# Two graph layers on one core: where the products of the first linear stand among those of the aggregate

## The chip, the cores and the metric

The kernel runs on one core of a Trainium2 chip. The metric is the device time of one execution in microseconds. Before the change the median of three runs is 2444.21 us (2444.15 to 2444.86).

## The reference, cut to what matters

The input x has 16 batches of 1024 rows and 256 channels, all in float32. Layer 0 is an attention over a weighted graph, with a residual and a layer normalisation; the change does not touch it. Layer 1, on its result x, is:

```python
A_norm = A + jnp.eye(n)
deg = A_norm.sum(0) + A_norm.sum(1) - jnp.diagonal(A_norm)
dinv = rsqrt(deg)
A_hat = A_norm * dinv[:, None] * dinv[None, :]
agg = jnp.einsum('nm,bmd->bnd', A_hat, x)          # the aggregate
h   = relu(batchnorm(agg @ W1.T + b1))             # the first linear: 256 -> 512
out = batchnorm(h @ W2.T + b2)                     # the second linear: 512 -> 256
x   = layernorm(x + out)
```

The batch normalisations take their statistics over all 16 x 1024 rows, so h can be scaled only once the first linear of every batch is done.

## The kernel before, in words

The kernel first works through layer 0, then through layer 1 in three stages: aggregate and first linear of every batch; second linear of every batch; normalisation, residual and output. The change lies in the first of these, the loop at L1636 over the batches b = 1 to 15. (The aggregate of batch 0 is made earlier, by `aggregate_first`; the linear of batch 15 comes after the loop, as plain products, L1673 to L1690.)

Both the aggregate and the linear are made with seven products in place of eight (the Strassen-Winograd scheme). `products` (L637) writes it once for both: three accumulating banks of PSUM, called a, b and c, and seven steps, in the order p1, p6, p2, p7, p5, p4, p3. Each step is some matmuls and the reading of the bank afterwards by one instruction:

- p1: bank a, then ScalarE copies it (L656). p2 adds to bank a, and ScalarE copies it to the first quarter of the output (L667 in the aggregate, L669 with a bias in the linear).
- p6: bank b, then an add on VectorE (L646 in the aggregate, L648 in the linear). p7 and p4 add to bank b, each followed by another such add.
- p5 and p3, on bank c:

```python
def p5():
    t["c"] = bank(f"c_{name}")
    mm(5, t["c"], True)
    nc.vector.tensor_add(out[3], t["c"], t["u3"])    # L679

def p3():
    mm(3, t["c"], False)                             # adds to the same bank
    nc.vector.tensor_add(out[1], t["c"], t["u2"])    # L687
```

A product that adds to a bank has to come after the instruction that read it.

In the aggregate (`aggregate`, L1541, matmuls at L1558) a step has four matmuls 128x128 by 128x512 in float32; each shows as two MATMUL records in the profile. Its left operands are the batch's x1l and sums of it, x1S, which GpSimd makes two batches ahead (`x1_sums`, L1533, at L692 to L695), when the aggregate that last used the buffer has ended. In the linear (`linear1`, L1566, matmuls at L1590) a step has one such matmul, and there are two groups g of seven steps for each batch: 14 products. After each group come four batch statistics on VectorE (L1599), and after the second the store of h to DRAM from GpSimd's queue (L1602). Before any of its products, `linear1(b)` issues four sums of the aggregate's result on VectorE, called tT (`right_sums`, L697, at L699 to L702); the p4, p5, p6 and p7 of the linear use them.

What sets the order: on TensorE, ScalarE and VectorE the order of instructions is the order in which the Python code issues them (`manual_schedule`, L1508); each engine works through its own queue. In the loop, each step of the aggregate of batch b is followed by products of the linear of batch b - 1, taken from the list `lin` by `run_linear(lin, k)` (L1622): k products, then whatever stands in the list before the next product (statistics, the store). Behind the aggregate's last step, p3, the loop calls `linear1(b)` for the next pass, and with it the four sums, and only then `run_linear`. In batch 1 the apply step of the last layer normalisation (`last_apply`), the last store of x1 and the load and sums of batch 2 follow the aggregate's first step. After batch 1 VectorE also computes the range of the denominators (L1608 to L1611), and after batch 2 one small matmul (L1615) follows.

PSUM has eight banks of 128x512 here, given out in turn (`bank`, L1519); the temporaries of the linear have one buffer each (`temps("h")`), tT and x1S two.

Of the kernel before, what the change touches and what calls it, by code (L numbers as in the profile page):

```python
# [515 lines left out]
def fast_path(  # L516
# [120 lines left out]
    def products(name, bank, out, mm, temps, bias):  # L637

        t = {}

        def add(dst, ps, src, b):
            if b is None:
                nc.vector.tensor_add(dst, ps, src)  # L646
            else:
                nc.vector.scalar_tensor_tensor(dst, ps, b, src, op0=ALU.add, op1=ALU.add)  # L648

        up, low = bias or (None, None)  # L650

        def p1():
            t["a"] = bank(f"a_{name}")
            mm(1, t["a"], True)
            t["p1"] = temps("p1", name)
            nc.scalar.copy(t["p1"], t["a"])  # L656

        def p6():
            t["b"] = bank(f"b_{name}")
            mm(6, t["b"], True)  # L660
            t["u2"] = temps("u2", name)
            add(t["u2"], t["b"], t["p1"], up)

        def p2():
            mm(2, t["a"], False)
            if up is None:
                nc.scalar.copy(out[0], t["a"])  # L667
            else:
                nc.scalar.activation(out[0], t["a"], AF.Identity, bias=up)  # L669

        def p7():
            mm(7, t["b"], False)
            t["u3"] = temps("u3", name)
            add(t["u3"], t["b"], t["p1"], low)
# [6 lines that stand above are left out]
        def p4():  # L681
            mm(4, t["b"], False)
            add(out[2], t["b"], t["p1"], low)

        def p3():
            mm(3, t["c"], False)
            nc.vector.tensor_add(out[1], t["c"], t["u2"])  # L687

        return [p1, p6, p2, p7, p5, p4, p3]
# [7 lines left out]
    def right_sums(eng, T, b11, b12, b21, b22):  # L697

        eng.tensor_tensor(T[0], b12, b11, ALU.subtract)  # L699
        eng.tensor_tensor(T[1], b22, T[0], ALU.subtract)  # L700
        eng.tensor_tensor(T[2], b22, b12, ALU.subtract)
        eng.tensor_tensor(T[3], b21, T[1], ALU.subtract)  # L702
# [32 lines left out]
    with (  # L735
# [545 lines left out]
        def load_x1l(b):  # L1281
            x1l[b] = xp.tile([P, NCH, C], F32, tag="x", name=f"x1l_{b}")
            nc.sync.dma_start(x1l[b], x1_chunks[b])
# [28 lines left out]
        with tc.manual_schedule(  # L1312
# [70 lines left out]
            for j in range(len(bursts)):  # L1383
                b, u = j // PERB, j % PERB
# [127 lines left out]
    with (  # L1512
# [9 lines left out]
        def temps(k):  # L1522
            return lambda key, name: strt.tile([P, HALF], F32, tag=f"{key}{k}", name=f"{key}_{name}")
# [9 lines left out]
        def x1_sums(b):  # L1533
            x1S[b] = strs.tile([P, 4, NCH // 2, P], F32, tag="x1S", name=f"x1S_{b}")
            xt = x1l[b]
            left_sums(
                nc.gpsimd, [x1S[b][:, i] for i in range(4)],
                xt[:, M0, C0], xt[:, M1, C0], xt[:, M0, C1], xt[:, M1, C1],
            )

        def aggregate(b):  # L1541
            pool, tag = (aggp, "agg") if b % 2 else (xTp, "xT")
            t = agg[b] = pool.tile([P, CC, N], F32, tag=tag, name=f"agg_{b}")
            xt, S, aT = x1l[b], x1S[b], aht["T"]

            def mm(k, ps, start):
                for i in range(NCH // 2):
                    lo, hi = aht[i], aht[i + NCH // 2]
                    left, right = {
                        1: (xt[:, i, C0], lo[:, H0]),  # L1550
                        2: (xt[:, i + NCH // 2, C0], hi[:, H0]),
                        3: (S[:, 3, i, :], hi[:, H1]),
                        4: (xt[:, i + NCH // 2, C1], aT[:, 3, i, :]),
                        5: (S[:, 0, i, :], aT[:, 0, i, :]),
                        6: (S[:, 1, i, :], aT[:, 1, i, :]),
                        7: (S[:, 2, i, :], aT[:, 2, i, :]),
                    }[k]
                    nc.tensor.matmul(  # L1558
                        ps, left, right, start=(start and i == 0), stop=(i == NCH // 2 - 1),
                        skip_group_check=True,  # L1560
                    )

            out = (t[:, 0, H0], t[:, 0, H1], t[:, 1, H0], t[:, 1, H1])
            return products(f"agg{b}", bank, out, mm, temps("a"), None)

        def linear1(b):  # L1566
            t = agg.pop(b)
            ht = hp.tile([P, HC, N], F32, tag="h", name=f"hw_{b}")
            tT = strs.tile([P, 4, HALF], F32, tag="tT", name=f"tT_{b}")
            right_sums(  # L1570
                nc.vector, [tT[:, i, :] for i in range(4)],
                t[:, 0, H0], t[:, 0, H1], t[:, 1, H0], t[:, 1, H1],
            )
            steps = []
            for g in range(2):
                up, low = g, 2 + g

                def mm(k, ps, start, g=g):
                    f0 = slice(g * P, (g + 1) * P)
                    f1 = slice(C + g * P, C + (g + 1) * P)  # L1580
                    left, right = {
                        1: (w1T[:, 0, f0], t[:, 0, H0]),
                        2: (w1T[:, 1, f0], t[:, 1, H0]),
                        3: (wS[:, 3, f0], t[:, 1, H1]),
                        4: (w1T[:, 1, f1], tT[:, 3, :]),
                        5: (wS[:, 0, f0], tT[:, 0, :]),
                        6: (wS[:, 1, f0], tT[:, 1, :]),
                        7: (wS[:, 2, f0], tT[:, 2, :]),
                    }[k]
                    nc.tensor.matmul(ps, left, right, start=start, stop=True, skip_group_check=True)  # L1590

                places = ((up, H0, 0), (up, H1, 1), (low, H0, 0), (low, H1, 1))
                out = [ht[:, k, hs] for k, hs, _ in places]
                bias = (cols["b1"][:, up : up + 1], cols["b1"][:, low : low + 1])
                steps += products(f"h{b}_{g}", bank, out, mm, temps("h"), bias)

                def stats(places=places, out=out):
                    for (k, _, half), o in zip(places, out):
                        nc.vector.bn_stats(bn1_st[:, k, 2 * b + half, :], o)  # L1599

                steps.append(stats)
            steps.append(lambda: nc.gpsimd.dma_start(h_d[b], ht))  # L1602
            return steps
# [18 lines left out]
        def run_linear(steps, k):  # L1622
            while steps and k:
                name = steps[0].__name__
                steps.pop(0)()
                k -= name.startswith("p")
            while steps and not steps[0].__name__.startswith("p"):
                steps.pop(0)()
# [4 lines left out]
            w1T[:, 0, F0], w1T[:, 1, F0], w1T[:, 0, F1], w1T[:, 1, F1],  # L1633
        )
        lin = linear1(0)
        for b in range(1, B):  # L1636
            if 1 < b < B - 1:
                load_x1l(b + 1)
                x1_sums(b + 1)
            elif b == B - 1:  # L1640
                h0 = []
                for i in range(2):
                    t = xp.tile([P, 2, N], F32, tag="x", name=f"hl_0_{i}")
                    nc.sync.dma_start(t, h_d[0][:, 2 * i : 2 * i + 2, :])
                    h0 += [t[:, 0, :], t[:, 1, :]]
            steps = aggregate(b)
            for i, step in enumerate(steps):
                step()
                if i == len(steps) - 1 and b < B - 1:
                    later = linear1(b)  # L1650
                if b > 1 or i > 0:
                    run_linear(lin, 3 if b == 1 and i in (3, 5) else 2)
                if b == 1 and i == 0:
                    last_apply()
                    nc.scalar.dma_start(x1_chunks[B - 1], x_last)
                    load_x1l(2)
                    x1_sums(2)
            lin = later
            if b == 1:
                denominators_range()  # L1660
            if b == 2:
                denominators_good()
# [399 lines left out]
```

## Time and profile before

| What | Value |
| --- | --- |
| median of three runs | 2444.21 us |
| the profiled execution | 2444.04 us |
| its span, first to last instruction | 2442.3 us |
| busy TensorE, VectorE, ScalarE, GpSimd | 98%, 76%, 51%, 19% of the span |
| mean granted TensorE clock | 0.997 |
| the loop of batches 1 to 15 | 1593.15 to 2140.74 us |
| distance of two batches in it, from batch 4 on | 36.42 us |

The busy shares are averages over the whole span. A line of the profile gives an instruction's line in the kernel (L1590), the engine, the tile written and the tiles read (`b_h<-tT,wS`: bank b of the linear, from tT and wS), and durations in us. In names, `a_agg`, `b_agg` and `c_agg` are the banks of the aggregate, `a_h`, `b_h` and `c_h` those of the linear; `u_h` and `p_h` are its temporaries, `hw` its output. PEld is TensorE's loading of weights, which runs beside its matmuls. A matmul's end is modelled, so the distance of two starts says more than a duration.

### The profile page before, as it was taken

What the parts mean: (1) busy time and instruction counts of PE and PEld (TensorE: products, weight loads), DVE (VectorE), ACT (ScalarE), POOL (GpSimd) and SP (SyncE); (2) the same over time, 40 slices, a digit from 0 to 9 for tenths busy, and PEclk for the clock granted to TensorE, in tenths of its full rate; (3) what the DMA queues carried; (4) which work ended last, traced back from release to release, by engine and by line L of the source; (5) the groups of instructions that cost most, each with busy time, mean ns of one, the idle gap of its engine ahead of it and who ended that gap; (6) DMA issues with size and microseconds to landing.
All of it is one profiled execution on the core that took longest, in us unless ns stands there. A gap on an engine that the chain in (4) does not pass through costs nothing.

```text
span 2442.3 us, 32486 instructions
## 1 busy us (share of the span) xinstructions
PE 2401.4 (98%) x12294; PEld 1015.7 (42%) x12294; DVE 1860.5 (76%) x2561; ACT 1239.0 (51%) x1539; POOL 462.8 (19%) x467
## 2 busy tenths in 40 slices
PE   9999999999999999999999999999999999999996
PEld 5343443443434434434344343344444444444444
DVE  5688878878888788788888888955566556479978
ACT  7376675765765756657657667420110111144568
POOL 0021112111211211112112112422122122010026
PEclk9999999999999999999999999999999999999999
DMA  5124232332242332332322326321221221265558
GB/s 164 40 40 87 56 50 70 69 52 65 41 81 57 49 79 61 53 70 53 66 62 40 87 46 92 90 103 69 86 103 69 88 102 69 86 222 177 180 202 357
DMA packets 437877, 221.96 MB, mean 91 GB/s; under 512 B 361552, under 2 KB 411216, under 8 KB 431568
## 3 DMA queue, kind: packets, MB, share of 16 engines
q1 hardware_dynamic: 418400, 169.20, 28.2%
q0 software_dynamic: 2528, 33.57, 3.3%
q10 hardware_dynamic: 16784, 17.04, 2.1%
q8 instruction: 98, 1.61, 0.3%
q14 instruction: 67, 0.55, 0.1%
HBM read 136.06 MB, written 83.69 MB: 90 GB/s over the span
## 4 chain that ended last, share of the span: by engine, by line
PE 86%; DVE 9%; ACT 2%; DMA 1%; issue 1%; POOL 0%; POOLq 0%; DVEq 0%; ACTq 0%
PE ps L1053 18%; PE po L1074 18%; PE pgb L885 7%; PE b_agg L1558 4%; PE pga L885 4%; PE c_agg L1558 4%; PE pk L982 4%; PE b_o L1766 3%; PE pv L995 3%; PE a_agg L1558 2%; PE b_h L1590 2%; PE pgc L885 2%; PE pgd L885 2%; PE c_o L1766 2%; PE a_o L1766 2%; PE c_h L1590 2%
## 5 line engine op out<-in xcount | busy, mean ns | idle before, releaser
L1058 ACT ACTIVATE p<-ps 128x1024 f32<-128x1024 f32 x512 | 497.2, 1021 | 183.8 <-PE ps L1053 146.0
L1084 DVE TENSOR_TENSOR acc<-acc,p 128x1024 f32<-128x1024 f32 x384 | 499.9, 1302 | 53.4 <-ACT p L1058 28.5
L1053 PE MATMUL ps<-qT,kT 64*64 64x512 f32 x4096 | 488.1, 592 | 0.3 <-ACT p L1058 0.3
L1074 PE MATMUL po<-p,v 64*64 64x512 f32 x4096 | 485.3, 589 | 0.0
L1149 POOL TENSOR_TENSOR o<-o,r_all 128x512 f32<-128x512 f32 x62 | 94.8, 1540 | 1162.3 <-DVE r_all L1143 989.0
L1074 PEld LDWEIGHTS po<-p,v 64*64 64x64 f32 x4096 | 158.2, 133 | 281.2 <-issue 274.3
L1053 PEld LDWEIGHTS ps<-qT,kT 64*64 64x64 f32 x4096 | 151.5, 133 | 286.8 <-issue 249.1
L836 DVE SCALAR_TENSOR_TENSOR wg<-wg,adj_s 128x1024 f32<-128x1024 f32 x128 | 149.6, 1216 | 17.6 <-ACT wg L832 17.6
L827 ACT ACTIVATE wg<-crow,ccol 128x1024 f32<-128x1024 f32 x128 | 146.8, 1147 | 0.0
L832 ACT ACTIVATE wg<-wg 128x1024 f32<-128x1024 f32 x128 | 136.0, 1062 | 0.9
L995 PE MATMUL pv<-kvw_s,xT 128*128 128x256 f32 x512 | 125.1, 387 | 0.0
L982 PE MATMUL pk<-xT,kvw_s 128*128 128x512 f32 x256 | 121.9, 598 | 3.1 <-ACT drow L1128 3.1
L995 PEld LDWEIGHTS pv<-kvw_s,xT 128*128 128x128 f32 x512 | 95.7, 191 | 50.3 <-issue 14.2
L895 ACT ACTIVATE qT<-qT 128x512 f32<-128x512 f32 x60 | 37.4, 630 | 156.1 <-DVE qT L898 145.3
L885 PE MATMUL pgb<-wg,S 128*128 128x512 f32 x240 | 111.0, 605 | 0.0
L885 PE MATMUL pga<-wg,x 128*128 128x512 f32 x240 | 109.6, 599 | 0.7 <-ACT qT L908 0.7
L1558 PE MATMUL a_agg<-ahT,x1l 128*128 128x512 f32 x240 | 108.1, 593 | 0.7 <-ACT agg L1300 0.7
L1150 POOL TENSOR_TENSOR x<-x,o 128x512 f32<-128x512 f32 x62 | 107.8, 1749 | 2.4
L1558 PE MATMUL b_agg<-aT,x1S 128*128 128x512 f32 x240 | 107.9, 592 | 0.0
L656 ACT COPY p_agg<-a_agg 128x512 f32<-128x512 f32 x15 | 8.8, 585 | 183.4 <-PE a_agg L1558 183.4
L692 POOL TENSOR_TENSOR x1S<-x1l 128x512 f32<-128x512 f32 x15 | 19.4, 1297 | 353.6 <-PE c_agg L1558 349.6
L1082 DVE TENSOR_TENSOR acc<-p,p 128x1024 f32<-128x1024 f32 x64 | 77.3, 1208 | 7.5 <-ACT p L1058 7.5
(230 smaller groups left out, 3468.5 us busy)
## 6 DMA issues: line engine op xcount, KB each, us to landing
h<-hw POOLq DMA_DIRECT2D x16, 2048.0 KB, 6.7
hl<-h SPq DMA_DIRECT2D x32, 1024.0 KB
x<-x ACTq DMA_DIRECT2D x16, 1024.0 KB
x1l<-x SPq DMA_DIRECT2D x16, 1024.0 KB
xf<-x SPq DMA_DIRECT2D x16, 1024.0 KB
o<-oS SPq DMA_DIRECT2D x62, 256.0 KB
o<-o SPq DMA_DIRECT2D x248, 64.0 KB
x<-in_x_dram SPq DMA_DIRECT2D x15, 1024.0 KB
```

What stands on the lines that cost most here:

```text
L827: nc.scalar.activation(w, s["crow"], AF.Abs, bias=s["ccol"][:, n : n + 1])
L832: nc.scalar.activation(w, w, AF.Tanh, scale=0.5)
L836: nc.vector.scalar_tensor_tensor(w, w, 1.0, adj_s[:, n, :], op0=ALU.subtract, op1=ALU.mult)
L885: nc.tensor.matmul(ps, left, right, start=(start and i == 0), stop=(i == NCH // 2 - 1), skip_group_check=True,)
L982: nc.tensor.matmul(ps, kvw_s[:, c, kc * P : (kc + 1) * P], s["xT"][:, c, hs], start=(c == 0), stop=(c == CC - 1),)
L995: nc.tensor.matmul(pt[:, j * C : (j + 1) * C], s["xT"][:, c, n * P : (n + 1) * P], kvw_s[:, c, C : 2 * C], start=(c == 0), stop=(c == CC - 1),
L1053: nc.tensor.matmul(ps[kh * D : (kh + 1) * D, hd * HALF : (hd + 1) * HALF], kT[r, pr, ks], qT[r, pr, qh * HALF : (qh + 1) * HALF], start=Tr ...
L1058: nc.scalar.activation(p, ps, AF.Exp)
L1074: nc.tensor.matmul(g["po"][kh][hd * D : (hd + 1) * D, :], s["v"][r, m, h * D : (h + 1) * D], p[r, hd * HALF : (hd + 1) * HALF], start=(m = ...
L1084: nc.vector.tensor_add(g["acc"], g["acc"], p)
L1558: nc.tensor.matmul(ps, left, right, start=(start and i == 0), stop=(i == NCH // 2 - 1), skip_group_check=True,)
L1766: nc.tensor.matmul(ps, left, right, start=(start and i == 0), stop=(i == 1), skip_group_check=True,)
```

## The change

Only the number of the linear's products behind each of the seven steps of the aggregate is changed. Before, no product followed the first step of batch 1, three followed its fourth and sixth, and two every other step. After, the counts are written out: a row for batch 1 and a row for all later batches. The sum is 14 in each, as before.

| behind the aggregate's | p1 | p6 | p2 | p7 | p5 | p4 | p3 |
| --- | --- | --- | --- | --- | --- | --- | --- |
| batch 1, before | 0 | 2 | 2 | 3 | 2 | 3 | 2 |
| batch 1, after | 0 | 1 | 2 | 3 | 2 | 3 | 3 |
| later batches, before | 2 | 2 | 2 | 2 | 2 | 2 | 2 |
| later batches, after | 1 | 2 | 2 | 2 | 2 | 2 | 3 |

In the later batches the products of the first group are p1 / p6, p2 / p7, p5 / p4, p3 behind the first four steps, and those of the second p1, p6 / p2, p7 / p5, p4, p3 behind the last three. Before, it was p1, p6 / p2, p7 / p5, p4 / p3 with the second group's p1 / p6, p2 / p7, p5 / p4, p3.

```diff
         lin = linear1(0)
+        counts = ((0, 1, 2, 3, 2, 3, 3), (1, 2, 2, 2, 2, 2, 3))
         for b in range(1, B):
...
             steps = aggregate(b)
             for i, step in enumerate(steps):
                 step()
                 if i == len(steps) - 1 and b < B - 1:
                     later = linear1(b)
                 if b > 1 or i > 0:
-                    run_linear(lin, 3 if b == 1 and i in (3, 5) else 2)
+                    run_linear(lin, counts[b > 1][i])
                 if b == 1 and i == 0:
                     last_apply()
```

## The prediction

> **What bounds the kernel now.** I read the page first, then the chain of waits, then TensorE's timeline through the stage that the change touches, then VectorE's beside it.
>
> ```profile
> span 2442.3 us, 32486 instructions
> PE 2401.4 (98%) x12294; PEld 1015.7 (42%) x12294; DVE 1860.5 (76%) x2561; ACT 1239.0 (51%) x1539; POOL 462.8 (19%) x467
> PE 86%; DVE 9%; ACT 2%; DMA 1%; issue 1%; POOL 0%; POOLq 0%; DVEq 0%; ACTq 0%
> ```
>
> TensorE (PE) is busy 98% of the span, so the question is only where it still waits, and where it will wait. The loop over batches 1 to 15 runs from the first aggregate product at 1593.15 us to the plain products at 2140.74 us: 547.6 us. A step of four aggregate products takes 3.43 us (1740.42 to 1743.86), so one product takes 0.858 us; the 28 + 14 of a batch take 42 x 0.858 = 36.05 us. In TensorE's timeline the starts of successive batches lie 36.42 us apart from batch 4 on: 0.37 us too much. The same timeline shows where it goes (columns: start, duration, instruction):
>
> ```profile
> 1749.01 1.02 PE L1590 MATMUL a_h<-agg,w12T 128*128 128x512 f32 x2
> 1750.14 1.13 PE L1590 MATMUL b_h<-tT,wS 128*128 128x512 f32 x2
> 1751.10 1.45 PE L1558 MATMUL a_agg<-ahT,x1l 128*128 128x512 f32 x3
> ```
>
> p2 of the linear starts at 1749.01, so p7 is due at 1749.87. It starts at 1750.14, and what follows starts 0.96 us later instead of 0.86: 0.37 us lost. The list of waits names the cause, the add of p6:
>
> ```profile
> PEld b_h L1590 <- DVE u_h L648: 13.5, 13, 2.3
> ```
>
> VectorE (DVE) reaches that add late, because of what stands ahead of it in its queue:
>
> ```profile
> 1738.91 0.69 DVE L687 TENSOR_TENSOR agg<-c_agg,u_agg 128x512 f32<-128x512 f32 x1 [2.74 <-PE c_agg L1558]
> 1739.63 1.14 DVE L699 TENSOR_TENSOR tT<-agg 128x512 f32<-128x512 f32 x1
> 1740.81 1.64 DVE L700 TENSOR_TENSOR tT<-agg,tT 128x512 f32<-128x512 f32 x1
> 1742.37 1.75 DVE L701 TENSOR_TENSOR tT<-agg 128x512 f32<-128x512 f32 x1
> 1744.05 1.75 DVE L702 TENSOR_TENSOR tT<-agg,tT 128x512 f32<-128x512 f32 x1
> 1745.72 0.74 DVE L648 SCALAR_TENSOR_TENSOR hw<-b_h,col_b,p_h 128x512 f32<-128x512 f32 x1
> 1746.38 0.67 DVE L687 TENSOR_TENSOR hw<-c_h,u_h 128x512 f32<-128x512 f32 x1
> 1746.98 2.46 DVE L1599 BATCH_NORM_STATS2 bn_st<-hw 128x6 f32<-128x512 f32 x4
> 1749.36 0.73 DVE L648 SCALAR_TENSOR_TENSOR u_h<-b_h,col_b,p_h 128x512 f32<-128x512 f32 x1
> ```
>
> From the add that ends the aggregate (L687) VectorE works without a gap: four right sums for the next batch (1739.63 to 1745.72, 6.09 us), two adds, four statistics, and only then the late add at 1749.36. In this order nothing that TensorE needs early stands behind the sums. In batch 14 the sums are short, and no wait follows:
>
> ```profile
> 2103.90 0.69 DVE L699 TENSOR_TENSOR tT<-agg 128x512 f32<-128x512 f32 x1
> ...
> 2106.44 0.74 DVE L648 SCALAR_TENSOR_TENSOR hw<-b_h,col_b,p_h 128x512 f32<-128x512 f32 x1
> ```
>
> **What the Trainium skill says.** "PSUM — Partial Sum Buffer", section "Engine vs sequencer instructions": VectorE's queue is strictly first in, first out, and matmuls complete in program order. The trace agrees: the add at 1749.36 starts only when the statistics end. "SBUF — State Buffer", "Who interferes with whom": a VectorE instruction with two SBUF inputs contends with a GpSimd instruction that reads SBUF. The trace agrees: the sums take 1.14 to 1.75 us each beside GpSimd's x1S sums (1738.97 to 1745.24), and 0.68 to 0.69 us in batch 14, where GpSimd has none. "TensorE: Matmul & The Clock Gate", Part 1: TensorE's clock halves after an idle window of about 3.4 us and returns after a busy one; Part 4 adds that transposes don't count as busy in the same way. The trace shows one such drop, in the last stage (columns: stretch, length, busy of five engines, granted clock, DMA):
>
> ```profile
> 2352.20:2355.60 3.40, 1.11 (x8) 0.92 (x8) 2.56 (x7) 3.29 (x3) 0.55 (x1) 1.00 0.93 390
> 2355.60:2356.00 0.40, 0.00 (x0) 0.00 (x0) 0.27 (x1) 0.40 (x1) 0.00 (x0) 0.68 0.92 389
> 2358.00:2359.00 1.00, 1.00 (x2) 0.23 (x1) 0.99 (x3) 1.00 (x1) 0.00 (x0) 0.50 0.00 0
> 2359.00:2359.40 0.40, 0.40 (x3) 0.20 (x2) 0.38 (x2) 0.40 (x2) 0.00 (x0) 0.80 0.00 0
> ```
>
> After 2.88 us of idle time behind a few transposes the clock is 0.50 from about 2355.7 to 2359.1, some 3.4 us, and a pair that otherwise takes 1.02 us takes 1.84.
>
> **The change part by part.** No instruction is added or removed; products of the linear move, with the adds and copies that they issue, past products of the aggregate. The order of instructions of the changed kernel shows it on TensorE and VectorE; on SyncE and GpSimd the order stays, and so do the store of h, at the end of the linear, and the loads of x1l.
>
> 1. p6 moves from behind the aggregate's p1 to behind its p6. Its add then ends by about 10.6 us of the batch (below) and p7, now behind the aggregate's p2, is due at 15 x 0.858 = 12.9: the wait goes. Worth 1.76 us in batch 2 (where VectorE also does the range of the denominators: p7 starts 1.66 late and loses 0.10 on restarting), 0.33 in batch 3, 0.37 x 11 = 4.07 in batches 4 to 14: 6.2 us. Batch 15 has none now.
>
> 2. The second p5 moves from in front of the aggregate's p3 to behind it. This is the step that decides. p5 writes bank c, the add L679 reads it, and p3 then accumulates into the same bank, so p3 has to wait for L679. Before, L679 stood ahead of the four sums in VectorE's queue. Now the sums are issued when the aggregate's p3 is, and the last three products after them: L679 stands behind the sums, and TensorE's next work, p3 and the whole next batch, behind L679. From the row of batch 4, counted from the end of the aggregate's p3 (1738.71): VectorE is through the sums at 1745.72, 7.01 us; L679 takes 0.69; the handover is 0.05 (1750.09 to 1750.14); the next batch starts 0.96 after p3: 8.71 us. Without a wait it would start after 3 x 0.858 = 2.57. The stall is 6.14 us. Sums beside GpSimd's come in batches 1 to 13: 13 x 6.14 = 79.8 us. In batch 14: L687 starts 0.20 after the product, the sums end 3.27 after that (2103.17 to 2106.44), so 0.20 + 3.27 + 0.69 + 0.05 + 0.96 - 2.57 = 2.6 us. In batch 15 there are no sums; p3 is due 0.86 us after p5's end and L679 needs 0.20 + 0.69 + 0.05: 0.2 us with the restart.
>
> Is anything late next? After the stall VectorE does two adds and four statistics, to about 3.4 us into the next batch (p3's add starts 0.2 after it, 0.69, then 2.46); the aggregate's p6 ends at 7.7 and the linear's p6 at 8.6, so their adds come in time. ScalarE's copy of p1 waits for the add of p4, as it does now (1.93 us), and is done before p6's add needs it. The other groups, two products after a step, have their adds one aggregate step ahead of the next user: nothing, as long as that cover of 3.43 us stays; without it 0.2 us each.
>
> 3. Batch 1 has its own row. Its groups of three put p7, p5, p4 together and p6, p2, p7 together: a product waits for an add that started a product earlier. Each loses some 0.25 us (0.20 + the two adds, 0.69 + 0.75, less 1.72 minus 0.86, gives 0.14 late after waiting and 0.10 for restarting), against 0.29 lost there now: +0.2 us.
>
> 4. The clock. 13 gaps of about 6.03 us are new; no gap in this stage now exceeds 1.5 us. Lower bound, an estimate from the 3.4 us seen: if only a window that lies wholly in the gap counts, it ends between 3.41 and 6.03 us into it, in 2.62 of 3.41 phases (77%); the slow time lasts one window, on average 1.31 us of it still idle, so 2.1 us of work at half speed, 1.05 us lost, 0.8 over all phases. Upper bound: if a window with little work doesn't restore the clock, the slow stretch is two windows, and the period, 36.05 + 6.14 = 42.19, is drawn to the next multiple of the window, 13 x 3.413 = 44.37 (a batch that starts later in the window loses less): 2.18 us lost. The trace can't tell them apart. Zero is the outer bound, if such gaps don't trip it at all. I take the middle of 0.8 and 2.18, 1.5 us: 13 x 1.5 = 19.5 us. Batch 14's gap of 2.5 us I cost at nothing; at most 1.7, half a window.
>
> Sum: 79.8 + 2.6 + 0.2 + 0.2 - 6.2 = +76.6 us of waits, + 19.5 of clock = +96.1. The profiled execution took 2444.04 us (span 2442.3, with 1.7 around it), 0.2 below the median of 2444.21; so 2444.2 + 96.1 = 2540.3 us.
>
> **The rivals.** (a) The stall, but the clock stays at full speed: 2444.2 + 76.6 = 2520.8. For it: the only drop in the trace came among transposes, and where a window falls is unknown. Against: 6.03 us is twice the gap that tripped it. (b) Not slower: the sums don't delay L679, so that only step 1 counts, 2444.2 - 6.2 = 2438.0. It decides at L679's place: L687 ends 0.89 after the aggregate's p3 and p3 of the linear is due at 1.72, so L679 must start by about 0.98; sums longer than 0.1 us in front of it make a wait. They take 6.09, or 2.54 in batch 14. For (b) speaks that the wait of step 1 really goes; but it would need L679 ahead of L699, and the order shows it behind L702. (c) The clock locks fully: 76.6 + 13 x 2.18 = 104.9, 2549.1; this belongs to the likeliest case's own range.
>
> **How the numbers follow.** Stall with a slower clock (0.8 to 2.18 us a gap, 2531 to 2549, some more before it settles): 0.68. Stall alone: 0.27. Faster: 0.03. Sums that are mostly hidden, within 0.2%: 0.02. The range takes in (a) with 2 us below it and goes to 2556 for a lock with a late start: 2518 to 2556. 0.2% (4.9 us) is about what a measurement can tell from no change. Faster 0.03, same 0.02, slower 0.95.
>
> **What would show it.** In the profile after, in this stage: c_h of L1590 waiting for DVE hw L679, 14 or 15 times, about 6 us each but for the last; the wait for u_h L648 gone from the list; batches 42 to 44.4 us apart; the granted clock below 1.00 in it. A period of 42.2 at clock 1.00 makes (a) right. Wrong in the mechanism: no wait at L679, or a period below 37 us.

## The result, and the profile after

The changed kernel takes 2550.39 us (median of 6 runs, 2548.49 to 2551.08) against 2444.14 us before (6 runs): 1.0434 times the time, 95% interval 1.0422 to 1.0446. The forecast was 2540.3 with a range of 2518 to 2556; the direction, the place and the stall were right, and one term, the clock, came out at its upper bound.

The profiled execution took 2549.18 us. The head of its page:

```profile
span 2547.4 us, 32473 instructions
PE 2430.9 (95%) x12294; PEld 1026.0 (40%) x12294; DVE 1862.4 (73%) x2561; ACT 1239.0 (49%) x1539; POOL 462.7 (18%) x467
PEclk9999999999999999999999999998989899999999
```

The same number of TensorE instructions is busy 29.5 us longer (2430.9 against 2401.4), which no added wait can do: they ran slower. The row PEclk, the granted clock in tenths, has eights in three slices of the changed stage. The loop of batches 1 to 15 now runs from 1592.90 to 2246.05 us, 653.2 us instead of 547.6: 105.6 us more, all of the 105.1 by which the span grew (the rest of the kernel gives half a microsecond back).

The list of TensorE's waits (instruction, what it waited for, total, times, longest) names the stall:

```profile
PE c_h L1590 <- DVE hw L679: 78.3, 14, 5.9
```

and the list of the weight loads has hardly anything left of the old wait, 1.7 us in place of 13.5:

```profile
PEld c_h L1590 <- DVE hw L679: 90.7, 15, 6.7
PEld b_h L1590 <- DVE u_h L648: 1.7, 2, 0.9
```

(The two totals of c_h are the same waits, seen by the matmul and by its weight load; they are not added.) VectorE's timeline in batch 10, from the add that ends the aggregate:

```profile
1981.29 0.69 DVE L687 TENSOR_TENSOR agg<-c_agg,u_agg 128x512 f32<-128x512 f32 x1 [2.68 <-PE c_agg L1558]
1982.02 1.14 DVE L699 TENSOR_TENSOR tT<-agg 128x512 f32<-128x512 f32 x1
1983.19 1.63 DVE L700 TENSOR_TENSOR tT<-agg,tT 128x512 f32<-128x512 f32 x1
1984.75 1.75 DVE L701 TENSOR_TENSOR tT<-agg 128x512 f32<-128x512 f32 x1
1986.42 1.74 DVE L702 TENSOR_TENSOR tT<-agg,tT 128x512 f32<-128x512 f32 x1
1988.08 0.68 DVE L679 TENSOR_TENSOR hw<-c_h,u_h 128x512 f32<-128x512 f32 x1
```

L679, the add that reads bank c, is last in the row. TensorE's timeline at the same place:

```profile
1981.95 1.02 PE L1590 MATMUL b_h<-tT,w12T 128*128 128x512 f32 x2
1988.81 2.08 PE L1590 MATMUL c_h<-agg,wS 128*128 128x512 f32 x2 [5.85 <-DVE hw L679]
1990.68 4.90 PE L1558 MATMUL a_agg<-ahT,x1l 128*128 128x512 f32 x8
1995.42 1.02 PE L1590 MATMUL a_h<-agg,w12T 128*128 128x512 f32 x2
```

p3 starts 0.05 us after L679 ends, 6.00 us later than the 1982.81 that follows from p4's start. Then it takes 2.08 us for what takes 1.02 elsewhere, and the step of four products behind it 4.90 instead of 3.60. The granted clock says why (columns: stretch, its length, busy of five engines, granted clock, DMA share, GB/s):

```profile
1982.80:1986.30 3.50, 0.17 (x1) 0.00 (x0) 3.47 (x3) 0.00 (x0) 3.42 (x3) 1.00 0.00 0
1986.60:1988.80 2.20, 0.00 (x0) 0.00 (x0) 2.20 (x3) 0.00 (x0) 1.01 (x1) 0.50 0.00 0
1988.80:1993.20 4.40, 4.39 (x5) 1.85 (x6) 2.89 (x5) 0.00 (x0) 0.57 (x1) 0.50 0.00 0
1993.40:1996.80 3.40, 3.40 (x10) 1.49 (x9) 0.60 (x2) 0.87 (x2) 0.00 (x0) 1.00 0.95 400
```

The clock falls to half while TensorE waits and stays there for some 4.5 us of work (1988.81 to about 1993.3). Read in slices of 0.1 us, the slow stretch of every one of batches 1 to 13 is 6.83 us long, and they begin 44.37 us apart. The distances between the starts of the aggregate's p3 show how the period is drawn to that value: 43.89, 44.35, 44.15, 44.26, 44.32, 44.34, then 44.36 to 44.38 in every batch. 6.83 is two times 3.413, and 44.37 is 13 times 3.413; 3.413 us, the length of the shortest slow stretches in these traces, is called a window in what follows.

Batch 14, whose sums have no GpSimd work beside them, waits less, and still pays for the clock:

```profile
2203.80 1.02 PE L1590 MATMUL b_h<-tT,w12T 128*128 128x512 f32 x2
2207.15 1.12 PE L1590 MATMUL c_h<-agg,wS 128*128 128x512 f32 x2 [2.33 <-DVE hw L679]
2208.11 5.29 PE L1558 MATMUL a_agg<-ahT,x1l 128*128 128x512 f32 x8
```

### The profile page after: what moved, and what is told of

It is laid out like the page before. It is cut to its first block, busy times and chain, and to the rows that moved or that the text cites. A ratio compares the mean times of both kernels' runs of the same rounds, so it can differ in the third digit from the quotient of the medians.

```text
span 2547.4 us, 32473 instructions
## 1 busy us (share of the span) xinstructions
PE 2430.9 (95%) x12294; PEld 1026.0 (40%) x12294; DVE 1862.4 (73%) x2561; ACT 1239.0 (49%) x1539; POOL 462.7 (18%) x467
## 4 chain that ended last, share of the span: by engine, by line
PE 88%; DVE 8%; ACT 2%; DMA 1%; issue 0%; POOL 0%; DVEq 0%; POOLq 0%; ACTq 0%
PE ps L1053 18%; PE po L1074 17%; PE pgb L885 6%; PE b_agg L1558 6%; PE a_agg L1558 5%; PE pga L885 4%; PE c_agg L1558 4%; PE pk L982 3%; PE b_o L1767 3%; PE b_h L1590 3%; PE pv L995 2%; PE c_h L1590 2%; PE pgc L885 2%; PE pgd L885 2%; PE a_h L1590 2%; PE a_o L1767 2%
## 5 line engine op out<-in xcount | busy, mean ns | idle before, releaser
L1084 DVE TENSOR_TENSOR acc<-acc,p 128x1024 f32<-128x1024 f32 x384 | 500.0, 1302 | 53.3 <-ACT p L1058 28.4
L1558 PE MATMUL a_agg<-ahT,x1l 128*128 128x512 f32 x240 | 125.4, 671 | 0.7 <-ACT agg L1300 0.7
L1590 PE MATMUL c_h<-agg,wS 128*128 128x512 f32 x60 | 44.5, 834 | 78.3 <-DVE hw L679 78.3
L648 DVE SCALAR_TENSOR_TENSOR u_h<-b_h,col_b,p_h 128x512 f32<-128x512 f32 x60 | 45.1, 751 | 98.7 <-PE b_h L1590 98.7
L646 DVE TENSOR_TENSOR u_agg<-b_agg,p_agg 128x512 f32<-128x512 f32 x30 | 20.7, 692 | 125.5 <-PE b_agg L1558 125.5
```

Source lines behind the costliest of these rows:

```text
L1084: nc.vector.tensor_add(g["acc"], g["acc"], p)
L1558: nc.tensor.matmul(ps, left, right, start=(start and i == 0), stop=(i == NCH // 2 - 1), skip_group_check=True,)
```

## The experiments

**The theory** had two parts: the whole stall comes from one product, the second group's p5, whose add L679 now stands behind the four sums; and the rest is the halved clock after the gap, with a period drawn to whole windows. **The rivals**: the general shift of the products (p6 too, or three in a row) is what costs; the loss above the stall is a fixed price of restarting; the clock costs a fixed amount per stall. Seven kernels, each against runs of the kernel before on the same chip.

**1. p5 in front again (p5_ahead).**

```diff
-        counts = ((0, 1, 2, 3, 2, 3, 3), (1, 2, 2, 2, 2, 2, 3))
+        counts = ((0, 1, 2, 3, 2, 4, 2), (1, 2, 2, 2, 2, 3, 2))
```

> The changed kernel with its last two groups cut differently: the second group's p5 goes back in front of the aggregate's p3 (rows 0, 1, 2, 3, 2, 4, 2 and 1, 2, 2, 2, 2, 3, 2). p6 stays where the change put it. Theory (only p5 behind the sums does harm): L679 is ahead of the sums again, both the new stall and the old wait at u_h are gone, batches 36.05 us apart, clock 1.00; 2444.1 - 6.2 + 0.2 = 2438.1 us. Rival (moving p6, or the pairs of products behind one add, costs as well): clearly above 2440, with waits at u_h or p_h in each batch.

Measured: 2437.54 us (2437.2 to 2439.24), 0.9975 of before, interval 0.9965 to 0.9985. The batches are 36.05 us apart in this trace (36.37 once, where the small matmul of the denominators stands), which is the 42 products without a gap. In VectorE's timeline L679 is ahead of the sums:

```profile
1732.80 0.69 DVE L679 TENSOR_TENSOR hw<-c_h,u_h 128x512 f32<-128x512 f32 x1
1736.23 0.69 DVE L687 TENSOR_TENSOR agg<-c_agg,u_agg 128x512 f32<-128x512 f32 x1 [2.74 <-PE c_agg L1558]
1736.96 1.15 DVE L699 TENSOR_TENSOR tT<-agg 128x512 f32<-128x512 f32 x1
```

So the shift of p6 and of everything else in the change is harmless, and worth the 6 us that the old wait cost. This version is faster than both kernels, than the one before by 0.25%.

**2. Only p5 behind (p5_behind_only).**

```diff
-        counts = ((0, 1, 2, 3, 2, 3, 3), (1, 2, 2, 2, 2, 2, 3))
+        counts = ((0, 2, 2, 3, 2, 2, 3), (2, 2, 2, 2, 2, 1, 3))
```

> The kernel before with one product moved: the second group's p5 goes behind the aggregate's p3 (rows 0, 2, 2, 3, 2, 2, 3 and 2, 2, 2, 2, 2, 1, 3); p6 stays behind the aggregate's p1. Theory: this product alone makes the whole difference; TensorE waits about 5.9 us at c_h for L679 in 13 batches, the period is drawn to 44.37 us, 2550 us within 3. Rival (the whole shift of the products by one does it, p5 being a part): well below, 2480 to 2530.

Measured: 2549.05 us (2548.58 to 2549.81), 1.0431 (1.0415 to 1.0447). TensorE's waits have the same line as in the changed kernel:

```profile
PE c_h L1590 <- DVE hw L679: 78.3, 14, 5.9
```

One product of 0.86 us, moved past one step, makes the whole difference. The old wait for u_h L648 is gone from the list here too, although p6 stays where it was: TensorE's stall gives VectorE the time to reach that add. So the changed kernel would have lost that wait without the move of p6.

**3. The same order on TensorE, the sums later on VectorE (sums_last).**

```diff
-                if i == len(steps) - 1 and b < B - 1:
-                    later = linear1(b)
                 if b > 1 or i > 0:
                     run_linear(lin, counts[b > 1][i])
+                if i == len(steps) - 1 and b < B - 1:
+                    later = linear1(b)
```

> The changed kernel, its products where the change put them, but with the call of linear1(b), and so the four sums on VectorE, issued after the last three products of the group and their adds and statistics. TensorE's order is that of the changed kernel; only VectorE's differs. Theory (L679 behind the sums is the whole cause): p3 follows p5's add by one product only and waits some 0.2 us, 14 times, 2.8 us; no gap of more than 0.2 us, clock 1.00; the sums, now free of GpSimd's for the most part, are done before the next batch's p6 needs them; 2444.1 - 6.2 + 0.2 + 2.8 = 2440.9 us. Rival (three products in a row behind the aggregate's p3 are late by themselves, since p5, p4 and p3 hang on each other): above 2480.

Measured: 2441.63 us (2440.97 to 2442.1), 0.9991 (0.9982 to 0.9999); 36.24 us a batch, 0.19 above the bare work. VectorE now does the adds first and the sums last, at full rate, since GpSimd's are over by then:

```profile
1736.41 0.69 DVE L679 TENSOR_TENSOR hw<-c_h,u_h 128x512 f32<-128x512 f32 x1 [0.17 <-PE c_h L1590]
1737.27 0.75 DVE L648 SCALAR_TENSOR_TENSOR hw<-b_h,col_b,p_h 128x512 f32<-128x512 f32 x1 [0.17 <-PE b_h L1590]
1738.32 0.69 DVE L687 TENSOR_TENSOR hw<-c_h,u_h 128x512 f32<-128x512 f32 x1 [0.30 <-PE c_h L1590]
1738.93 2.46 DVE L1599 BATCH_NORM_STATS2 bn_st<-hw 128x6 f32<-128x512 f32 x4
1741.31 0.67 DVE L699 TENSOR_TENSOR tT<-agg 128x512 f32<-128x512 f32 x1
```

TensorE's order is that of the changed kernel to the instruction, and 109 us are gone. It is the place of L679 in VectorE's queue, not the three products in a row.

**4. GpSimd's sums left out (no_x1S_sums).**

```diff
-                x1_sums(b + 1)
+                x1S[b + 1] = x1S[1]
```

> The changed kernel without GpSimd's sums x1S from batch 3 on: the aggregates of these batches read the sums of batch 1 again, so that part of the computation is left out. VectorE's four sums then have no GpSimd work beside them. Theory (the stall is the sums' length, 6.09 us beside GpSimd and 2.54 without): in every batch the wait of batch 14, 2.6 us lost; 2444.1 - 6.2 + 0.4 + 14 x 2.6 = 2474.7 us, and up to 1.7 us a batch more where the clock falls for one window, 2498; about 2490. Rival (the sums' slow rate comes from PSUM or from the copies of ScalarE, not from GpSimd): 2550.

Measured: 2488.34 us (2488.3 to 2490.79), 1.0185 (1.0169 to 1.02). The third sum takes 0.684 us in the median instead of 1.743 (durations in ns: shortest, median, longest; first the changed kernel, then this run):

```profile
L701 DVE TENSOR_TENSOR tT<-agg x15: 684/1743/1746, 1596.9 to 2205.2; 128x512 f32<-128x512 f32 x15
L701 DVE TENSOR_TENSOR tT<-agg x15: 681/684/690, 1596.2 to 2143.1; 128x512 f32<-128x512 f32 x15
```

The batches are 38.64 or 40.34 us apart, never anything else apart from one of 38.96 with the small matmul: 2.6 us of stall each, and another 1.7 where the clock falls, for one window of 3.41 us, after 8 of the stalls. The length of the stall is the length of the sums, and more than half of that is GpSimd's company.

**5. The gap filled (filled_gap).** Six matmuls into a bank that nobody reads, two in batch 14 (`fill(k)` issues k of them; its definition is left out here):

```diff
-                    run_linear(lin, counts[b > 1][i])
+                    if i == len(steps) - 1 and b < B - 1:
+                        run_linear(lin, 2)
+                        fill(6 if b < B - 2 else 2)
+                        run_linear(lin, 1)
+                    else:
+                        run_linear(lin, counts[b > 1][i])
```

> The changed kernel with six more matmuls (two in batch 14) on TensorE between the linear's p4 and p3 of the second group, where it waits; they write a bank that nobody reads, and wait for nothing. That is 80 more matmuls, 69 us of work, all inside gaps. Theory (the halved clock costs some 28 us beside the stall): the clock stays at 1.00, the batches are 42.2 us apart, and the kernel becomes FASTER by 28 us: 2521 us. Rival (the loss above 6.14 us a batch is a fixed cost of restarting after a wait): 2550 us or more, batches 44.4 us apart.

Measured: 2520.60 us (2519.52 to 2520.7), 1.0312 (1.0296 to 1.0328). TensorE does 69 us more work and the kernel is 29.8 us faster than the changed one. The timeline of one batch:

```profile
1881.88 5.31 PE L1625 MATMUL fill<-ahT,w12T 128*128 128x512 f32 x12
1887.90 1.13 PE L1590 MATMUL c_h<-agg,wS 128*128 128x512 f32 x2 [0.71 <-DVE hw L679]
1888.86 3.60 PE L1558 MATMUL a_agg<-ahT,x1l 128*128 128x512 f32 x8
```

p3 waits for L679 as before, but only 0.71 us idle, and what follows takes 3.60 us again; the clock over the whole stage is 1.00:

```profile
1590.00:2215.00 625.00, 614.43 (x1424) 268.98 (x1423) 316.19 (x421) 61.52 (x101) 102.37 (x81) 1.00 0.20 76
```

The batches are 42.17 to 42.19 us apart (42.50 once, where the small matmul of the denominators stands): 36.05 + 6.14 = 42.19, the stall alone. A fixed price of restarting after the wait would still be there, and it is not, beyond the 0.10 us that the 6.14 includes. A price that grew with the length of the wait would be gone too; that it is the clock is read from the granted share, 0.50 behind the stalls of the changed kernel and 1.00 here. This splits the result: 76.5 us of waits (2520.6 - 2444.1, the old wait that went already taken off) and 29.8 of clock.

**6. One more matmul in each of batches 2 to 13 (one_more_matmul)**, away from the gap.

```diff
+                if i == 3 and 1 < b < B - 2:
+                    fill(1)
```

> The changed kernel with one more matmul (0.86 us) behind the aggregate's p7 group in each of batches 2 to 13, into a bank that nobody reads: 12 x 0.858 = 10.3 us more work on the engine that bounds the stage. Theory (the period is locked to 13 clock windows of 3.413 us): a batch restarts later in the window, loses less to the slow clock, and stays 44.37 us; 2550 us within 2. Rival (the clock costs a fixed 2.2 us a stall): 45.2 us a batch, 2560.7 us.

Measured: 2557.22 us (2556.97 to 2558.83), 1.0465 (1.0449 to 1.0481). Neither: 6.8 us of the 10.3 show. The periods tell what happened: 46.38, 45.17, 44.78, 44.57, 44.48, 44.42, then 46.10, 45.24, 44.81, 44.59, 44.48. They fall towards 44.37 and don't reach it; then the batch has come so late in the window that the clock falls one window later, for one window at first, and when a slow stretch lasts two windows again, its period is long (46.10). The slow stretches begin 44.37 us apart within such a row and 47.78 (14 windows) at the slip. The lock asks for 44.37 - 43.05 = 1.32 us of loss; the smallest seen is 44.42 - 43.05 = 1.37.

**7. Half a matmul more (half_more_matmul)**, 256 columns instead of 512.

> As the run with one more matmul, but each of the 12 is half as long (256 columns, 0.43 us): 5.2 us more work on TensorE. Theory (periods are drawn to 13 clock windows, 44.37 us, as long as the loss that this needs, here 44.37 - 42.19 - 0.43 = 1.75 us, is one that the slow clock can give; the run with one more matmul asked for 1.32, just below what it gave at least, 1.37): all absorbed, 2550 us within 1.5, batches 44.37 us apart. Rival (a fixed loss of 2.18 us a stall): 2555.6 us, 44.8 us apart.

Measured: 2552.02 us (2551.03 to 2552.46), 1.0442 (1.0426 to 1.0458): 1.6 us above the changed kernel, a little outside the 1.5 that was expected, and well below the 5.2 of the added work. The batches come to 44.37 us again (44.53, 44.67, 44.31, 44.35, 44.36, then 44.37), and all 13 slow stretches are 6.83 us and start 44.37 apart. Between the aggregate's p3 of batch 1 and that of batch 14 the run needs 576.75 us, the changed kernel 575.89: 0.9 us of the 5.2. So the lock is real, within the losses that it can give.

## Why the prediction was right, and where its size was off

- **Step 1, the old wait goes: right in its size.** Forecast 6.2 us. With only this part of the change in effect (experiment 1) the kernel is 6.5 us faster than before (2437.5 against 2444.1). In the changed kernel the reason given, p6's new place, isn't needed: experiment 2 leaves p6 where it was, and the stall takes the wait away by itself.
- **Step 2, the stall: right.** Forecast 6.14 us a batch, 42.19 us a period without the clock; experiment 5 has 42.17 to 42.19. Batch 14: forecast 2.6; L679 ended 2207.10 and p3 started 2.49 us late, 2.6 with the restart. Batch 15: forecast 0.2, measured 0.19. Nothing was late behind the stall, as forecast: VectorE's statistics end 3.3 us into the next batch (1991.54 + 2.46 against 1990.68), and no wait for u_h follows.
- **Step 3, batch 1: small, as forecast**, some 0.4 us for a forecast of 0.2: up to the aggregate's p3 the batch loses 0.7 us beside its products, against 0.3 before.
- **The stalls together:** forecast +76.6 us, that is 2520.8; experiment 5, which keeps the stalls and takes the clock away, gives 2520.6.
- **Step 4, the clock: the term that was mis-sized.** I took the middle of two bounds, 1.5 us a gap or 19.5 in all, and nothing for batch 14. The upper bound is what happened: a period of 44.37 us, 2.18 us a gap. From batch 1's p3 to batch 14's the 13 periods hold 575.89 - 13 x 36.05 = 107.2 us of loss, less 79.8 of stall: 27.4 of clock, with the 0.3 of the small matmul in it (28.4 was the bound; the first batches, still on their way to the lock, lost less). Batch 14 lost 40.34 - 36.05 - 2.6 = 1.7, its stated bound too. Some 29 us in place of 19.5 is the 10 us by which the forecast was low.
- **What the choice of the middle overlooked.** The lower bound supposed that a single window brings the clock back, however little work is in it. The records decide against that. In the changed kernel the window in which TensorE resumes is up to 31% busy (batch 13: it runs from 2163.96 to 2167.37, work resumes at 2166.30), and the clock stays low for the next one. In the run with one more matmul 82% didn't bring it back (window 1948.16 to 1951.57, resumed at 1948.76) and 84% did (1903.79 to 1907.20, resumed at 1904.34). The wait itself puts the resumption late in its window, so two slow windows are the rule.
- **The transposes.** The prediction took from the Trainium skill ("TensorE: Matmul & The Clock Gate", Part 4) that transposes don't count as busy in the same way, and so held it in favour of rival (a) that the one drop before the change came among transposes. These runs speak against that here. The slow stretch in the last stage of the kernel before, 2355.7 to 2359.1, ended after one window; TensorE had resumed at 2356.19, and of the 3.0 us of work in that window the first 1.3 were transposes. Without them the window would be 47% busy, and 82% wasn't enough elsewhere. The first microseconds of experiment 3's trace are plainer: transposes start 0.21 us apart there, so at half the rate of the 0.11 in the last stage at full clock, and the clock is full from 8.81 us, after a window (5.40 to 8.81) of which transposes take the first 3.06 us. What the same page says in Part 1, a window of about 3.4 us, fits: the stretches are 3.41 and 6.83 us.
- **The rivals.** (a), the stall at full clock, needs something in the gap: it is experiment 5. (b), not slower, fell at L679's place, as the prediction said it would; experiment 3 moves just that and is back at 2441.6. (c), the lock, is what came: 2549.1 forecast, 2550.4 measured.

## What to carry to other kernels

When work is moved behind another engine's step, ask what the other engine has been given in the same place: here one product of 0.86 us was put behind 6.1 us of sums that nobody needed soon, because its bank is read by an add in the same queue. A stall of some microseconds on a busy TensorE can cost more than its length: here 5.85 us of waiting cost another 2.2, since the clock fell in it and came back only after a nearly full window of work. Where such a stall comes in a period, the upper bound of that loss is the better guess, for the period can settle there. And where a stall can't be removed, idle matmuls in it can be worth their place: experiment 5 gained 29.8 us by them.

## What the runs showed of the hardware that I had not expected

- The clock falls on fixed marks: in each of the nine traces every slow stretch begins a whole number of windows of 3.413 us after the one before it (12, 13, 14, 22, 23 or 74, for instance).
- The period of this loop locks to that window. Slow stretches of the changed kernel are 6.83 us in batches 1 to 13 and start 44.37 us apart, 13.00 windows; half a matmul more in each batch (0.43 us) leaves the period at 44.37, a whole one (0.86 us) breaks the lock.
- The way down and the way up are not alike. The clock fell after a window that was 35% busy (batch 14 of the changed kernel: window 2204.92 to 2208.33, idle from 2204.66 to 2207.15), and did not after one that was 42% busy (run with one more matmul: 1852.59 to 1856.00, idle from 1854.02). It came back after a window 84% busy and not after one 82% busy. The line is less sharp than these figures. A matmul's end is modelled: the two records of a product start 0.43 us apart and last 0.59 each, a difference of 5% of a window. One window 87% busy by the same reckoning did not bring the clock back (run with one more matmul, 1678.51 to 1681.92; it holds the small matmul of the denominators). And the clock fell after one 49% busy, 1.2 us of it transposes (experiment 3, 2346.94 to 2350.35). What counts as busy there stays open.
- An idle gap of 2.33 us is enough to lose 1.7 us to the clock, if it lies well in the window: 8 of the 14 gaps of this length in experiment 4, and the one in batch 14 of the changed kernel. In experiment 4 the window of each of the eight is 32 to 39% busy, and that of each of the other six 42 to 57%.
